# Summing rows, columns and the skip term on TensorE in a state-space output stage

## The chip, the cores and the metric

The kernel runs on one core of a Trainium2 chip. The metric is the device time of the whole program in microseconds. The core has a matrix engine (TensorE, "PE" in the profile, its weight loads "PEld"), VectorE ("DVE"), ScalarE ("ACT"), GpSimd ("POOL") and SyncE ("SP"), which here only issues DMAs. The engines run side by side; each executes its own queue in order, and they wait for each other through semaphores. On-chip tiles lie in SBUF; matmul results lie in PSUM, in banks of 128 partitions by 512 fp32 numbers. All data are fp32.

## The reference, cut to what matters

The input is `x` of 8 images, 96 channels, 128 by 128. Layer 0 normalizes it in groups, runs a convolutional LSTM over its rows and adds the result to `x`. Layer 1 normalizes again, splits each image by a wavelet transform into a low band and three high bands of 64 by 64, sends the low band through a four-direction state-space scan, weighs the high bands by an attention vector, transforms back and adds to its input. The change is in the last lines of the scan (`L` is 4,096, `D_INNER` is 192):

```python
out_y = jnp.moveaxis(ys, 0, -1) + Ds.reshape(K, D_INNER)[None, :, :, None] * xs
inv_y = jnp.flip(out_y[:, 2:4], -1)
wh_y = jnp.swapaxes(out_y[:, 1].reshape(Bn, D_INNER, w, h), 2, 3).reshape(Bn, D_INNER, L)
invwh_y = jnp.swapaxes(inv_y[:, 1].reshape(Bn, D_INNER, w, h), 2, 3).reshape(Bn, D_INNER, L)
y = out_y[:, 0] + inv_y[:, 0] + wh_y + invwh_y
y = jnp.moveaxis(y.reshape(Bn, D_INNER, h, w), 1, -1)
y = _layernorm(y, out_norm_w, out_norm_b)
y = y * jax.nn.silu(z)
return y @ out_proj_w.T
```

Each position of an image therefore gets the sum of the scans along rows (both senses), the scans along columns (both senses), and a skip term: the scan's input times the sum of the four `Ds`. The sum over the 192 inner channels is then layer-normalized, gated by `silu(z)` and projected to 96 channels.

## The kernel before, in words

The program has three stages. First, layer 0 (lines 87 to 224). Second, the scans of all images in turn. Third, a tail, which finishes the last image.

**The scans.** An image has 16 chunks of 512 positions: eight forward (`p` is 0), then the same eight backward. Rows lie in partitions 0 to 63 and columns in 64 to 127 of every scan tile, 64 of the 192 channels at a time (`q` is 0 to 2). A chunk has 24 slots. In a slot two of the 16 states are worked on, 1,024 elements a partition: GpSimd multiplies the input with the B rows (`product`, L1001), ScalarE makes the decays in one of two PSUM buffers (`decay`, L1012), VectorE scans (L1025) and multiplies with the C rows (L1191; every fourth slot GpSimd does it, L1199), and TensorE adds up the states by transposing products against the identity (`add_up`, L1039). SyncE loads B and C rows (`bt`, `ct`, L990) five blocks ahead into rotating tiles. The finished rows and columns go to DRAM as `y_d[b][0]` and `y_d[b][1]`.

**The background.** All other work of neighbouring images is done in the gaps between these instructions: the wavelet analysis and projections of image b+1 (`analysis`, L551), the output stage of image b-1 (`output`, L832) and its inverse transform (`synthesis`, L768). Each of these is a generator (a job) that yields, ahead of every step, its engine, a cost in us, how many rounds it must stay behind the step before (three or more count double), and what it takes or gives of the counted resources: three PSUM banks, twelve `short` tiles of 128 by 512, and some more (`free`, L481). `background` (L1132) is called up to twice a slot, after the scan and before the next one. It gives each engine a budget (TensorE 1.1 us, ScalarE 0.9, VectorE 0.7, GpSimd 1.3, SyncE without limit), and `write` (L488) lets jobs issue steps in order of rank until the budget is gone. Where the scan needs a job's result that has not been issued, `drain` (L538) issues with no limit until it has. All this happens when the program is built; on the chip every engine simply has a fixed order. Synthesis jobs of an image start only when all its output blocks are written out.

**The output stage.** `output` has eight jobs `block(j)` an image, one for each 512 positions, each after the one before. The 192 channels are two parts of 128 and 64 (`parts`). For each part, SyncE loads rows (`y`, L843), columns (`t`, L844), scan input (`u`, L845) and gate (`z`, L846); GpSimd adds columns to rows (L849); VectorE adds the skip term, `u` times the channel's `dsum` (L851). Then, for each part, TensorE multiplies both parts of the sum with `ceny` (identity minus 1/192), which takes the mean off (`pf`, L859); ScalarE squares it (L862) and VectorE multiplies it with the gate (L864). Two more products give the variance (`pv`, L868) and the projection (`po`, L876); ScalarE makes the reciprocal root (L871, L872), VectorE applies it (L879), a last product adds the projected norm bias (`pq`, L883 and L886), and SyncE stores 96 by 512 to `ll_d` (L888).

**Queues.** Loads and stores that SyncE issues stand in one queue; if one has to wait for its buffer, the `bt` and `ct` loads behind it wait too. The weights (`ceny`, `dsum`, `wow`) are made once, at lines 390 to 411. The step vectors' input `dt` of a chunk is loaded by `load_dt` (L926) into one of two buffers and read by three products (L943).

Of the kernel before, what the change touches and what calls it, by code (L numbers as in the profile page):

```python
# [7 lines left out]
F32 = mybir.dt.float32  # L8
# [9 lines left out]
DI = 192  # L18
# [38 lines left out]
def forward_kernel(ctx: ExitStack, tc: tile.TileContext, i, out):  # L57
# [173 lines left out]
    with ExitStack() as s:  # L231
# [163 lines left out]
        for part_i, (d0, m) in enumerate(parts):  # L395
            nc.sync.dma_start(ceny[0:m, part_i, d0:d0 + m], i["ident"][0:m, 0:m])
        nc.vector.tensor_scalar_add(ceny, ceny, -1.0 / DI)
        dsk = wp.tile([128, 2, 4], F32, name="dsk")
        dsum = wp.tile([128, 2], F32, name="dsum")
        onw = wp.tile([128, 2, 2], F32, name="onw")  # L400
# [2 lines left out]
        for part_i, (d0, m) in enumerate(parts):  # L403
            nc.sync.dma_start(dsk[0:m, part_i, :], i["DsT"][d0:d0 + m, :])
            nc.vector.tensor_reduce(dsum[0:m, part_i:part_i + 1], dsk[0:m, part_i, :], AX.X, ALU.add)
            nc.sync.dma_start(onw[0:m, part_i, 0:1], i["out_norm_w"][d0:d0 + m, :])
            nc.sync.dma_start(onw[0:m, part_i, 1:2], i["out_norm_b"][d0:d0 + m, :])
            nc.sync.dma_start(wo[0:m, part_i, :], i["woutT"][d0:d0 + m, :])
            for j in range(2):
                nc.vector.tensor_scalar_mul(wow[0:m, part_i, j, :], wo[0:m, part_i, :],  # L410
                                            onw[0:m, part_i, j:j + 1])

# [63 lines left out]
                    for r in self.give:  # L478
                        free[r] += 1

        free = dict(bank=3, short=NSHORT, raw=2, ph=2, wa=2, yf=2, dl=5)  # L481
        jobs = []
        now, at_slot = [0], [-1]

# [347 lines left out]
        def output(b, begin, end, after):  # L832

            def block(j):
                o = slice(512 * j, 512 * j + 512)
                ys, zs = [], []
                t, u = None, None
                for part_i, (d0, m) in enumerate(parts):
                    yield "SP", 0, (1 if part_i else 0), NONE, NONE
                    if part_i == 0:  # L840
                        t, u = short("t"), short("uo")
                    y, z = short("ysum"), short("zo")
                    nc.sync.dma_start(y[0:m], y_d[b][0, d0:d0 + m, o])  # L843
                    nc.sync.dma_start(t[0:m], y_d[b][1, d0:d0 + m, o])  # L844
                    nc.sync.dma_start(u[0:m], u_d[b][0, d0:d0 + m, o])  # L845
                    nc.sync.dma_start(z[0:m], sz_d[b][d0:d0 + m, o])  # L846
                    ys.append(y), zs.append(z)
                    yield "POOL", 1.3, 3, NONE, NONE
                    nc.gpsimd.tensor_add(y[0:m], y[0:m], t[0:m])  # L849
                    yield "DVE", 1.0, 2, NONE, NONE  # L850
                    nc.vector.scalar_tensor_tensor(y[0:m], u[0:m], dsum[0:m, part_i:part_i + 1], y[0:m],  # L851
                                                   ALU.mult, ALU.add)

                sq, g = (t, ys[1]), (u, ys[0])
                for part_i, (d0, m) in enumerate(parts):
                    yield "PE", 1.72, 1, BANK, NONE
                    pf = ps.tile([m, 512], F32, name="pf", tag="mm")
                    for k_i, (_, k) in enumerate(parts):
                        nc.tensor.matmul(pf, ceny[0:k, k_i, d0:d0 + m], ys[k_i][0:k],  # L859
                                         start=(k_i == 0), stop=(k_i == 1))  # L860
                    yield "ACT", 0.6, 2, NONE, NONE
                    nc.scalar.activation(sq[part_i][0:m], pf, AF.Square)  # L862
                    yield "DVE", 0.68, 2, NONE, BANK
                    nc.vector.tensor_mul(g[part_i][0:m], pf, zs[part_i][0:m])  # L864
                yield "PE", 1.72, 1, BANK, NONE
                pv = ps.tile([C, 512], F32, name="pv", tag="mm")
                for part_i, (d0, m) in enumerate(parts):
                    nc.tensor.matmul(pv, on[0:m, 0:C], sq[part_i][0:m], start=(part_i == 0), stop=(part_i == 1))  # L868
                yield "ACT", 1.3, 2, NONE, BANK
                rs, lo = sq  # L870
                nc.scalar.activation(rs[0:C], pv, AF.Ln, bias=eps[:C])  # L871
                nc.scalar.activation(rs[0:C], rs[0:C], AF.Exp, scale=-0.5)  # L872
                yield "PE", 1.72, 0, BANK, NONE
                po = ps.tile([C, 512], F32, name="po", tag="mm")
                for part_i, (d0, m) in enumerate(parts):
                    nc.tensor.matmul(po, wow[0:m, part_i, 0, :], g[part_i][0:m],  # L876
                                     start=(part_i == 0), stop=(part_i == 1))
                yield "DVE", 0.68, 2, NONE, BANK
                nc.vector.tensor_mul(lo[0:C], po, rs[0:C])  # L879
                yield "PE", 1.72, 1, BANK, NONE  # L880
                pq = ps.tile([C, 512], F32, name="pq", tag="mm")
                for part_i, (d0, m) in enumerate(parts):
                    nc.tensor.matmul(pq, wow[0:m, part_i, 1, :], zs[part_i][0:m],  # L883
                                     start=(part_i == 0), stop=(part_i == 1))
                yield "DVE", 0.68, 2, NONE, BANK
                nc.vector.tensor_add(lo[0:C], pq, lo[0:C])  # L886
                yield "SP", 0, 2, NONE, NONE
                nc.sync.dma_start(ll_d[b][:, o], lo[0:C])  # L888

            done = []  # L890
            for j in range(L // 512):
                done.append(add(begin + (end - begin) * j / (L // 512), block(j), after=[*after, *done[-1:]], urgent=300,
                                take=SHORT * 6, give=SHORT * 6))
            return done
# [31 lines left out]
        def load_dt(ci):  # L926
            b, p, c = chunks[ci]
            yield "SP", 0, 0, NONE, NONE
            dts[ci] = sp.tile([128, CH], F32, name="dt")
            nc.sync.dma_start(dts[ci], dt_d[b][:, c * CH:(c + 1) * CH])  # L930

        def softplus(ci, q):
# [5 lines left out]
            qc = (q + 1) % 3  # L938
            nc.sync.dma_start(du[0:64], u_d[b][0, 64 * q:64 * q + 64, cs])
            nc.sync.dma_start(du[64:128], u_d[b][1, 64 * qc:64 * qc + 64, cs])  # L940
            yield "PE", 0.86, 4, BANK, NONE
            pt = ps.tile([128, CH], F32, name="pt", tag="mm")
            nc.tensor.matmul(pt, dw[:, p, q, :], dts[ci], start=True, stop=True)  # L943
            yield "ACT", 0.62, 2, NONE, NONE
# [169 lines left out]

        now0, dt_job = [0], {}
        ends, att = analysis(0, 0, 0)
        dt_job[0] = add(0, load_dt(0), ends, urgent=1000)
        for q in range(3):
            prepare(0, q, ends)
            hasten(ready[0, q])  # L1120
# [19 lines left out]
        for s in range(total):  # L1140
# [18 lines left out]
            if slot == 0:  # L1159
# [11 lines left out]
                if ci + 1 < len(chunks):  # L1171
                    after = analysed[b + 1][0] if step + 1 == len(order) else []
                    now0[0] = now[0] - halves(s)
                    dt_job[ci + 1] = add(now[0], load_dt(ci + 1), after, urgent=1000)
                    for t in range(3):
                        prepare(ci + 1, t, after)
                if p == 1:
# [99 lines left out]
```

## Time and profile before

| what | value |
|---|---|
| median of three runs | 15,879.47 us (15,873.98 to 15,884.72) |
| the profiled execution's own time | 15,881.9 us |
| its span, first to last instruction | 15,880.1 us |
| mean granted TensorE clock | 0.877 |
| first scan starts, last scan ends | 3,567.9 us, 15,379.0 us |
| TensorE, VectorE, ScalarE, GpSimd busy | 12,017.8, 11,728.4, 8,726.4, 11,270.4 us |
| DMA | 2,239 MB, mean 141 GB/s |

In the rows below, a group is given as line, engine, operation, output and inputs, shapes and count; then its busy time in us, the mean of one instruction in ns, and the idle time of the engine just before, with what ended most of it. A row of a stretch gives start and end, its length, the busy time of PE, PEld, DVE, ACT and POOL with their instruction counts, the granted TensorE clock, the DMA engines' busy share and GB/s. A row of waits gives who waited for whom, total us, how often, and the longest. A timeline row gives start, duration, engine, line, operation and shapes. An fp32 matmul appears as two PE instructions. Shapes such as 64*128 are rows and columns of the weights.

### The profile page before, as it was taken

How to read it: one execution, taken by the hardware profiler on the slowest of the kernel's cores; microseconds unless marked ns; L12 is line 12 of the kernel's file. 1: busy time of each engine (PE TensorE's matmuls, PEld its weight loads, DVE VectorE, ACT ScalarE, POOL GpSimd, SP SyncE). 2: the span in 40 equal slices, each digit the busy share in tenths (PEclk: the TensorE clock that was granted, in tenths of full speed). 3: DMA queues.
4: the chain of work that ended last, by engine and by line, in shares of the span. 5: the costliest groups of instructions: out<-in, count | busy, mean ns of one | idle time of the engine just before them, and what ended most of it. 6: DMA issues, size and time to landing. Idle time of an engine off the chain costs nothing. (4 is left out here: it accounts for less than half of the span.)

```text
span 15880.1 us, 146749 instructions
## 1 busy us (share of the span) xinstructions
PE 12017.8 (76%) x42850; PEld 6570.4 (41%) x42850; DVE 11728.4 (74%) x8612; ACT 8726.4 (55%) x15473; POOL 11270.4 (71%) x9544
## 2 busy tenths in 40 slices
PE   2999999586776777777777777777777777766666
PEld 0444444234444444444444444444444444444432
DVE  4333333209999988998899889888998898899871
ACT  0444444236766665666566656655665566555440
POOL 1333333009899987997798889878987898799760
PEclk9999999788887988888888888888888898877876
DMA  7333333246767777776777777777777777766653
GB/s 166 72 73 72 71 64 66 55 93 167 166 145 164 173 162 157 172 178 153 158 176 170 156 166 174 167 159 164 176 167 156 165 175 164 154 148 145 143 113 78
DMA packets 2458101, 2239.33 MB, mean 141 GB/s; under 512 B 1322929, under 2 KB 1523058, under 8 KB 2457043
## 3 DMA queue, kind: packets, MB, share of 16 engines
q1 hardware_dynamic: 1313491, 2007.56, 54.7%
q10 hardware_dynamic: 1143808, 222.38, 8.5%
q8 instruction: 344, 5.64, 0.2%
q14 instruction: 458, 3.75, 0.1%
HBM read 1862.20 MB, written 367.03 MB: 140 GB/s over the span
## 5 line engine op out<-in xcount | busy, mean ns | idle before, releaser
L1001 POOL TENSOR_TENSOR xb<-du,bt 128x1024 f32<-128x1024 f32 x3072 | 7245.7, 2362 | 330.9 <-DMA bt<-bc_d 169.6
L1025 DVE TENSOR_TENSOR_SCAN da<-da,xb 128x1024 f32<-128x1024 f32 x2304 | 5262.9, 2284 | 377.2 <-ACT da L1012 356.7
L1012 ACT ACTIVATE da<-dl,av 128x512 f32<-128x512 f32 x6144 | 4249.6, 692 | 1044.7 <-DVE hc L1191 494.7
L1039 PE MATMUL py<-ident,hc 128*128 128x128 f32 x18432 | 2882.3, 308 | 2400.6 <-DVE hc L1191 2272.9
L1039 PEld LDWEIGHTS py<-ident,hc 128*128 128x128 f32 x18432 | 2402.5, 159 | 3526.6 <-issue 1478.3
L1191 DVE TENSOR_TENSOR hc<-da,ct 128x1024 f32<-128x1024 f32 x2304 | 2813.2, 1221 | 552.5 <-DMA ct<-bc_d 390.9
L181 PE MATMUL pg<-hx,wq 128*128 128x512 f32 x4608 | 2019.7, 592 | 0.0
L1199 POOL TENSOR_TENSOR xb<-xb,ct 128x1024 f32<-128x1024 f32 x768 | 1809.3, 2356 | 99.3 <-DVE xb L1025 45.6
L1152 ACT COPY carry<-da 128x2 f32<-128x2 f32 x2016 | 319.9, 159 | 2721.8 <-DVE hc L1191 2492.7
L1025 DVE TENSOR_TENSOR_SCAN xb<-da,xb 128x1024 f32<-128x1024 f32 x768 | 1750.1, 2279 | 60.9 <-ACT da L1012 48.3
L584 PE MATMUL pd<-ph,wa 128*128 128x512 f32 x2304 | 1223.2, 663 | 262.7 <-ACT ph L578 142.3
L811 PE MATMUL pd<-ph,wg 128*128 128x504 f32 (+1 forms) x2304 | 1214.1, 659 | 204.5 <-DMA ph<-ll_d 124.4
L181 PEld LDWEIGHTS pg<-hx,wq 128*128 128x128 f32 x4608 | 871.7, 189 | 1106.7 <-issue 1106.3
L198 POOL TENSOR_TENSOR x1b<-xb,hx 96x512 f32<-96x512 f32 x256 | 302.7, 1183 | 1369.7 <-DVE hx L197 1124.4
L186 ACT ACTIVATE gate<-pg,gbias 32x512 f32<-32x512 f32 x768 | 523.3, 681 | 1185.2 <-PE pg L181 1185.2
L644 PE MATMUL pc<-xp,wc 97*128 97x512 f32 x2304 | 1143.6, 627 | 3.4 <-ACT bcs L674 3.4
L1039 PE MATMUL py<-ident,xb 128*128 128x128 f32 x6144 | 1006.5, 318 | 142.4 <-POOL xb L1199 140.5
L1039 PEld LDWEIGHTS py<-ident,xb 128*128 128x128 f32 x6144 | 879.2, 167 | 543.2 <-issue 266.7
L192 DVE TENSOR_TENSOR gate<-gate,gate 96x512 f32<-96x512 f32 x256 | 186.7, 729 | 840.9 <-ACT gate L186 840.9
L584 PEld LDWEIGHTS pd<-ph,wa 128*128 128x128 f32 x2304 | 452.7, 212 | 745.2 <-issue 439.9
L811 PEld LDWEIGHTS pd<-ph,wg 128*128 128x128 f32 x2304 | 461.7, 215 | 677.5 <-issue 580.3
L178 PE MATMUL pg<-x,wq 128*128 128x512 f32 x1536 | 703.4, 594 | 14.7 <-POOL x L168 14.7
(179 smaller groups left out, 12317.9 us busy)
## 6 DMA issues: line engine op xcount, KB each, us to landing
bt<-bc_d SPq DMA_DIRECT2D x2048, 256.0 KB
ct<-bc_d SPq DMA_DIRECT2D x2048, 256.0 KB
raw<-x_d SPq DMA_DIRECT2D x384, 288.0 KB
xb<-in_x SPq DMA_DIRECT2D x64, 1536.0 KB
du<-u_d SPq DMA_DIRECT2D x768, 128.0 KB
wa<-wa_d SPq DMA_DIRECT2D x192, 384.0 KB
xs<-in_x SPq DMA_DIRECT2D x64, 1024.0 KB
x_d<-x1b SPq DMA_DIRECT2D x792, 64.0 KB
```

The lines of the kernel that those rows point to most:

```text
L178: nc.tensor.matmul(pg[m], wq[:, 3, m, :], xk[:, r, bs, 0:W], start=True, stop=False)
L181: nc.tensor.matmul(pg[m], wq[:, tap, m, :], hk[:, r, bs, tap:tap + W], start=False, stop=(tap == 2))
L186: nc.scalar.activation(gg[32 * m:32 * m + 32], pg[m][96:128], AF.Tanh, bias=gbias[96:128, m:m + 1])
L584: nc.tensor.matmul(pd, wa[:, 3 * ty + tx, :], ph[:, ty:ty + 8, tx:tx + W2], start=(ty == tx == 0), stop=(ty == 1 and tx == 2))
L644: nc.tensor.matmul(pc, wc[:, tap, d0:d0 + 128], xp[:, r + ty:r + ty + 8, tx:tx + W2], start=(tap == 0), stop=(tap == 8))
L811: nc.tensor.matmul(pd[:, :, c0:c1], wgs[g][:, 3 * ty + tx, :], ph[:, ty:ty + 8, c0 + tx - 1:c1 + tx - 1], start=(k == 0 and tx == 1), stop ...
L1001: nc.gpsimd.tensor_mul(xb, du.unsqueeze(1).to_broadcast([128, GN, CH]), bcts[k, 0])
L1012: nc.scalar.activation(das[s][:, j], inputs[ci, q][0], AF.Exp, scale=av[:, p, q, n0 + j:n0 + j + 1])
L1025: nc.vector.tensor_tensor_scan(h, da, xb, 0.0, ALU.mult, ALU.add)
L1039: nc.tensor.matmul(pys[key][:, 128 * t:128 * t + 128], hc[:, j, 128 * t:128 * t + 128], ident, is_transpose=True, skip_group_check=True, s ...
L1191: nc.vector.tensor_mul(hc, das[s], bcts[kb, 1])
L1199: nc.gpsimd.tensor_mul(xb, xb, bcts[pk, 1])
```

## The change: what it does

The three sums before the centring product are written into it. The product is linear, so `ceny` times (rows + columns + `dsum` times u) becomes five products that accumulate in one PSUM bank: `ceny` on rows, `ceny` on columns and `cend` on u for the first 128 channels, then one for the last 64 channels' rows and columns stacked in one tile (`yt`), and one for their u. `cend` is `ceny` with its rows scaled by `dsum`. A copy of the last 64 rows of `ceny`, and of `wow`, is put in partitions 64 to 127, where the stacked tiles need them; u and gate of the last 64 channels are stacked too (`uz`). L849 and L851 go. A block now issues its eight loads in one step, makes ten centring matmuls where it made four, and holds two PSUM banks (one for each part) until both parts are squared and gated. To make room for `cend`, the two `dt` buffers become one, with a resource that makes `load_dt` of the next chunk come after the third product of this one.

```diff
         nc.vector.tensor_scalar_add(ceny, ceny, -1.0 / DI)
+        nc.sync.dma_start(ceny[64:128, 1, :], ceny[0:64, 1, :])
+        cend = wp.tile([128, 2, DI], F32, name="cend")
...
             nc.vector.tensor_reduce(dsum[0:m, part_i:part_i + 1], dsk[0:m, part_i, :], AX.X, ALU.add)
+            nc.vector.tensor_scalar_mul(cend[0:m, part_i, :], ceny[0:m, part_i, :], dsum[0:m, part_i:part_i + 1])
...
+        nc.sync.dma_start(wow[64:128, 1, 1, :], wow[0:64, 1, 1, :])
...
-        free = dict(bank=3, short=NSHORT, raw=2, ph=2, wa=2, yf=2, dl=5)
+        free = dict(bank=3, short=NSHORT, raw=2, ph=2, wa=2, yf=2, dl=5, dt=1)
...
-                ys, zs = [], []
-                t, u = None, None
+                yield "SP", 0, 0, NONE, NONE
+                y, t, u, z = (short(n) for n in ("yo", "to", "uo", "zo"))
+                for tile_o, src in ((y, y_d[b][0]), (t, y_d[b][1]), (u, u_d[b][0]), (z, sz_d[b])):
+                    nc.sync.dma_start(tile_o, src[0:128, o])
+
+                yt, uz = short("yt"), short("uz")
+                for tile_o, lower, upper in ((yt, y_d[b][0], y_d[b][1]), (uz, u_d[b][0], sz_d[b])):
+                    nc.sync.dma_start(tile_o[0:64], lower[128:192, o])
+                    nc.sync.dma_start(tile_o[64:128], upper[128:192, o])
+
+                terms = ((0, 128, ceny, y), (0, 128, ceny, t), (0, 128, cend, u), (1, 128, ceny, yt), (1, 64, cend, uz))
+                sq, g, zs = (t, yt), (u, y), (z, uz[64:128])
+                pf = [None, None]
                 for part_i, (d0, m) in enumerate(parts):
-                    yield "SP", 0, (1 if part_i else 0), NONE, NONE
-                    if part_i == 0:
-                        t, u = short("t"), short("uo")
-                    y, z = short("ysum"), short("zo")
-                    nc.sync.dma_start(y[0:m], y_d[b][0, d0:d0 + m, o])
-                    nc.sync.dma_start(t[0:m], y_d[b][1, d0:d0 + m, o])
-                    nc.sync.dma_start(u[0:m], u_d[b][0, d0:d0 + m, o])
-                    nc.sync.dma_start(z[0:m], sz_d[b][d0:d0 + m, o])
-                    ys.append(y), zs.append(z)
-                    yield "POOL", 1.3, 3, NONE, NONE
-                    nc.gpsimd.tensor_add(y[0:m], y[0:m], t[0:m])
-                    yield "DVE", 1.0, 2, NONE, NONE
-                    nc.vector.scalar_tensor_tensor(y[0:m], u[0:m], dsum[0:m, part_i:part_i + 1], y[0:m],
-                                                   ALU.mult, ALU.add)
-
-                sq, g = (t, ys[1]), (u, ys[0])
+                    for n, (k_i, k, weights, rhs) in enumerate(terms):
+                        yield "PE", 0.86, (3 if part_i == n == 0 else 0), (BANK if n == 0 else NONE), NONE
+                        if n == 0:
+                            pf[part_i] = ps.tile([m, 512], F32, name="pf", tag="mm")
+                        nc.tensor.matmul(pf[part_i], weights[0:k, k_i, d0:d0 + m], rhs[0:k],
+                                         start=(n == 0), stop=(n == len(terms) - 1))
                 for part_i, (d0, m) in enumerate(parts):
-                    yield "PE", 1.72, 1, BANK, NONE
-                    pf = ps.tile([m, 512], F32, name="pf", tag="mm")
-                    for k_i, (_, k) in enumerate(parts):
-                        nc.tensor.matmul(pf, ceny[0:k, k_i, d0:d0 + m], ys[k_i][0:k],
-                                         start=(k_i == 0), stop=(k_i == 1))
-                    yield "ACT", 0.6, 2, NONE, NONE
-                    nc.scalar.activation(sq[part_i][0:m], pf, AF.Square)
-                    yield "DVE", 0.68, 2, NONE, BANK
-                    nc.vector.tensor_mul(g[part_i][0:m], pf, zs[part_i][0:m])
+                    yield "ACT", 0.6, (2 if part_i == 0 else 0), NONE, NONE
+                    nc.scalar.activation(sq[part_i][0:m], pf[part_i], AF.Square)
+                for part_i, (d0, m) in enumerate(parts):
+                    yield "DVE", 0.68, (2 if part_i == 0 else 0), NONE, BANK
+                    nc.vector.tensor_mul(g[part_i][0:m], pf[part_i], zs[part_i][0:m])
...
-                    nc.tensor.matmul(pq, wow[0:m, part_i, 1, :], zs[part_i][0:m],
+                    nc.tensor.matmul(pq, wow[128 - m:128, part_i, 1, :], zs[part_i],
...
-            dts[ci] = sp.tile([128, CH], F32, name="dt")
+            dts[ci] = sp.tile([128, CH], F32, name="dt", bufs=1)
...
-            yield "PE", 0.86, 4, BANK, NONE
+            yield "PE", 0.86, 4, BANK, (("dt",) if q == 2 else NONE)
...
-                    dt_job[ci + 1] = add(now[0], load_dt(ci + 1), after, urgent=1000)
+                    dt_job[ci + 1] = add(now[0], load_dt(ci + 1), after, take=("dt",), urgent=1000)
```

More of the change, by code (lines that the diff above doesn't have):

```diff
@@ L1116, in forward_kernel @@
         ends, att = analysis(0, 0, 0)
-        dt_job[0] = add(0, load_dt(0), ends, urgent=1000)
+        dt_job[0] = add(0, load_dt(0), ends, take=("dt",), urgent=1000)
         for q in range(3):
```

## The prediction

> **What bounds the kernel now.** I read the page first, for the busy shares and the costliest groups.
>
> ```profile
> PE 12017.8 (76%) x42850; PEld 6570.4 (41%) x42850; DVE 11728.4 (74%) x8612; ACT 8726.4 (55%) x15473; POOL 11270.4 (71%) x9544
> ...
> L1001 POOL TENSOR_TENSOR xb<-du,bt 128x1024 f32<-128x1024 f32 x3072 | 7245.7, 2362 | 330.9 <-DMA bt<-bc_d 169.6
> L1025 DVE TENSOR_TENSOR_SCAN da<-da,xb 128x1024 f32<-128x1024 f32 x2304 | 5262.9, 2284 | 377.2 <-ACT da L1012 356.7
> ...
> L1191 DVE TENSOR_TENSOR hc<-da,ct 128x1024 f32<-128x1024 f32 x2304 | 2813.2, 1221 | 552.5 <-DMA ct<-bc_d 390.9
> ```
>
> The shares are averages over three stages: the first layer (to about 3,100 us), the scans (3,568 to 15,379 us by the starts of L1025, 3,072 of them, 3.84 us each) and a tail of 501 us after the last scan. The output blocks sit in the last two: 56 of 64 in the scan stage, 8 in the tail. So the next view is one image's scan stage, cut where the output blocks lie (chunks 1 to 5 of image 2) and where the synthesis is bunched (chunks 11 and 12), and what VectorE waited for over that whole image.
>
> ```profile
> 6511.00:6945.60 434.60, 341.96 (x1375) 193.23 (x1376) 417.39 (x273) 298.10 (x559) 413.65 (x361) 0.89 0.73 173
> ...
> 7414.90:7633.70 218.80, 158.28 (x614) 90.11 (x613) 169.02 (x115) 112.98 (x217) 158.01 (x141) 0.86 0.71 148
> ...
> DVE hc L1191 <- DMA ct<-bc_d: 57.3, 17, 12.0
> DVE da L1025 <- ACT da L1012: 53.6, 26, 6.7
> DVE raw L817 <- PE pd L811: 22.7, 15, 4.2
> ```
>
> The columns are PE, PEld, DVE, ACT, POOL busy, clock, DMA share, GB/s. In the output chunks VectorE is busy 417 of 435 us: it sets the pace there, and what leaves its queue shortens them. In chunks 11 and 12 it is busy 169 of 219, and waits for C rows (ct) and for TensorE's synthesis products. GpSimd is nearly as full, but VectorE hardly waits for it.
>
> Third, the groups touched, in the whole execution, then VectorE's in the tail alone (15,385 to 15,630 us).
>
> ```profile
> L859 PE MATMUL pf<-ysum,ceny 128*128 128x512 f32 (+3 forms) x512 | 328.0, 744 | 98.4 <-DVE ysum L851 98.4
> ...
> L851 DVE SCALAR_TENSOR_TENSOR ysum<-uo,dsum,ysum 128x512 f32<-128x512 f32 (+1 forms) x128 | 200.0, 1562 | 105.7 <-POOL ysum L849 105.6
> ...
> L849 POOL TENSOR_TENSOR ysum<-ysum,t 128x512 f32<-128x512 f32 (+1 forms) x128 | 162.1, 1266 | 217.9 <-DMA t<-y_d 214.2 <-PE pf L859 3.1 <-issue 0.2
> ...
> L851 DVE SCALAR_TENSOR_TENSOR ysum<-uo,dsum,ysum 128x512 f32<-128x512 f32 (+1 forms) x16 | 11.9, 747 | 89.7 <-POOL ysum L849 89.7
> ```
>
> L851 takes 0.75 us alone and 1.68 us ((200.0 - 11.9)/112) while GpSimd works. An fp32 matmul is two instructions: x512 is 256 matmuls.
>
> Last, the tail's timeline on TensorE, and its clock.
>
> ```profile
> 15402.56 5.86 PE L859 MATMUL pf<-ysum,ceny 64*128 64x512 f32 x6 [1.97 <-DVE ysum L851]
> 15408.35 2.02 PE L868 MATMUL pv<-t,on 128*96 128x512 f32 x2
> 15410.31 2.02 PE L868 MATMUL pv<-ysum,on 64*96 64x512 f32 x2
> ...
> 15402.60:15420.00 17.40, 17.40 (x18) 3.39 (x18) 2.06 (x3) 2.50 (x4) 0.00 (x0) 0.50 0.00 0
> ```
>
> TensorE works without a break for 17.4 us of each 29.3-us block at half clock, 1.95 us a matmul: in the tail TensorE is the path.
>
> **The change part by part.**
>
> *Sums taken off GpSimd and VectorE, scan stage.* 112 L851 go: 188 us busy; an instruction starts 0.08 us before its predecessor's end (6583.31 + 1.66 against the next start at 6584.90), so 180 us of VectorE's queue. With them goes the wait for L849, 105.6 - 89.7 = 16 us. GpSimd's 112 x 1.27 = 142 us free no path. Sum: -196 us.
>
> *Matmuls added.* Four become ten. From matmul starts in the trace sorted by shape and clock, one instruction takes 0.43 us for 128 rows by 128 columns, 0.53 for 64 by 128, 0.48 for 64 columns; at half clock 0.85, 1.01, 0.91. Old: 3.9 us a block (7.6 at half clock); new: 8 x 0.43 + 0.09 + 2 x 0.53 + 10 x 0.48 = 9.4 us (18.1). At the scan stage's clock of 0.88 (a quarter of the time at half) that is 6.7 us more a block, 375 us in all, beside VectorE's work: chunks 1 to 5 leave TensorE 93 of 435 us idle and get six blocks, 40 us. What may show is the Square (L862): ScalarE would stand there if TensorE is late, with the next decays (L1012) queued behind it and VectorE's scan behind those. Today L862 waits 195.4 us for pf, of which the tail has 164.6 + 25.2: 6 us in the scan stage, so TensorE is on time. Bounds 0 and 56 x 3 = 170; I take +20, near today's row. The first matmul now waits for the loads where GpSimd did; of GpSimd's 217.9 us before L849 the tail has 217.3, so in the scan stage they have always landed: 0.
>
> *Loads.* Eight per block as before, same bytes, but issued in one go (8 x 0.45 = 3.6 us of SyncE against twice 1.8). B and C loads behind them come up to 1.8 us later: 0 to 100 us, +10 taken, since ct waits in these chunks are rare.
>
> *Order.* The planner puts everything else elsewhere. In the order written out for both kernels, image 2's last pf moves from chunk 9 to 6 and the store of its last block from slot 246 to 171; synthesis sums (L817) per chunk from chunk 8 on go from 0, 0, 3, 12, 7, 6, 8, 12 to 4, 4, 6, 6, 8, 4, 11, 5. Slots with 13 or more SyncE issues, where the ct waits of before sit, fall from 61 to 41. A third off 390.9 us of ct waits is 130; slots with 6 or more background matmuls rise from 65 to 90, so I take -100, with ends of +150 (the bunches of ScalarE work, behind 53.6 us of an image's waits, are as many as before and may fall worse) and -280 (half of the ct and pd waits of seven images, 80 us each). Two centring banks are now held together of three; that is in this order, and analysis still ends before the image does (slot 344 against 350).
>
> *One dt buffer, setup.* The order has dt loads at the same slots (22 of the chunk before to 5) and their last reader at 12 to 14 of it: 0; if a load came late the products of the next chunk would wait, a few us per chunk at most. Setup: two copies and two multiplies, 0.6 us an issue on SyncE: +1.
>
> *Tail.* Per block the first matmul starts about 3.8 us after the first load (L849 started 4.4 us after it) instead of 6.6. Then ten pf. [...] By the row all stays at half: 3.8 + 18.1 + 11.3 (pv, po, pq) + 1.6 (last sum, store) = 34.8 us, +44 for 8 blocks. But that run starts with 64-row and 64-column shapes, streaming 1.71 of 1.95 us. Sorted over the trace, 3.4-us steps at half clock with above 80% streaming of full shapes are followed by full clock in over 97 of 100, below 60% in none; full clock is lost only below 50%. The new block opens with four 128x128 matmuls, 6.8 us at half clock without gaps; the same shape in the synthesis got the full clock 3.6 and 4.8 us after a pause. So by the rule: 3.8 + 4.4 at half clock (2.6 matmuls) + 7.2 + 5.9 + 1.6 = 22.9 us, -51. I take the rule's, its shape being the nearest row.
>
> *Sum.* -196 + 20 + 10 - 100 + 1 - 51 = -316 on the span of 15,880: 15,564. The profiled run took 15,881.9 and the median is 15,879.5, so it carries over: **15,560 us**.
>
> **The rivals.**
> 1. *No gain from order, cold tail.* -196 + 44 + 60 (late Squares) = 15,788. For: the planner weighs no waits; against: the ct waits follow SyncE's crowded slots.
> 2. *The even synthesis takes half of those waits.* -280 in place of -100: 15,384. For: chunks 11 and 12 take 108 us each against 85 in chunks 3 to 5; against: 53.6 us of ScalarE waits per image stay.
> 3. *TensorE late, slower.* At L862 ScalarE stands until the tenth matmul, the decays behind it. It decides from 316/56 = 5.6 us a block on; at 8 us the time is 15,564 + 448 = 16,012. For: at half clock a block wants 18 us plus 0.21 x 8 per transposed slot, and the planner counts 8.6; against: such a backlog fills TensorE above 80% and so brings the full clock.
> 4. *It does nothing:* VectorE's freed time turns into waits for ct or decays; 15,870. Against: chunks 1 to 5, 96% busy.
>
> **How the numbers follow.** Sum as worked out 0.47 (15,470 to 15,650), rival 1 0.22, rival 2 0.15, rival 3 0.13, rival 4 0.03. A measurement tells 0.2% (32 us) from nothing. Faster 0.84, same 0.03, slower 0.13. Range: from rival 2 to a little above rival 1, 15,380 to 15,840; outside are rival 3, rival 4 and a little below.
>
> **What would show it.** L849 and L851 gone and 1,280 pf instructions; VectorE busy about 200 us less; chunks 1 to 5 still over 95% busy and some 14 us shorter; ct waits near 260 us; L862's waits in the scan stage under 40 us; tail blocks near 23 us with a clock that reaches 1.0 in each. Wrong if the waits for decays (L1012) grow by more than 200 us, or if the tail stays at 0.50.

## The result and the profile after

The changed kernel takes 15,697.77 us (median; 15,690.29 to 15,712.49), the kernel before 15,882.09 us beside it: a ratio of 0.9888, 95% interval 0.9875 to 0.9900. It is 1.1% faster, by 184 us where 320 were forecast. The profiled execution has a span of 15,702.6 us against 15,880.1, so 177.5 us are there to be found.

The page of the changed kernel, busy shares and the same three groups:

```profile
PE 12169.3 (77%) x43618; PEld 6616.4 (42%) x43618; DVE 11561.5 (74%) x8486; ACT 8727.7 (56%) x15473; POOL 11082.0 (71%) x9416
...
L1002 POOL TENSOR_TENSOR xb<-du,bt 128x1024 f32<-128x1024 f32 x3072 | 7238.8, 2360 | 332.2 <-DVE da L1026 167.1
L1026 DVE TENSOR_TENSOR_SCAN da<-da,xb 128x1024 f32<-128x1024 f32 x2304 | 5265.7, 2285 | 384.0 <-ACT da L1013 355.8
...
L1192 DVE TENSOR_TENSOR hc<-da,ct 128x1024 f32<-128x1024 f32 x2304 | 2816.4, 1222 | 535.4 <-DMA ct<-bc_d 365.6
```

VectorE's busy time fell by 167 us. The wait for C rows (`ct`), which the forecast put near 260 us, is 366: it hardly moved from 391.

The same stretches of image 2 as before, chunks 1 to 5 and then 11 and 12 (start and end, length, busy PE, PEld, DVE, ACT, POOL, clock, DMA share, GB/s):

```profile
6490.10:6923.90 433.80, 358.89 (x1445) 192.68 (x1444) 405.35 (x266) 295.51 (x557) 396.96 (x349) 0.93 0.75 181
7391.80:7603.00 211.20, 155.98 (x606) 92.03 (x605) 167.37 (x114) 118.66 (x226) 160.28 (x142) 0.85 0.71 148
```

In chunks 1 to 5 VectorE has 405 us of work where it had 417, yet the stretch is 0.8 us shorter, not 14: the share of busy time fell from 96% to 93%. Chunks 11 and 12 are 7.6 us shorter. The means over images 1 to 6 are steadier: chunks 1 to 5 take 433.2 us (437.3 before), chunks 11 and 12 together 213.1 (216.0), of which chunk 12 alone grew, from 107.5 to 115.4.

The whole tail before and after, in the same columns:

```profile
15379.00:15880.00 501.00, 313.91 (x462) 97.90 (x460) 68.06 (x97) 28.80 (x47) 20.12 (x16) 0.63 0.31 74
15253.40:15702.60 449.20, 303.59 (x560) 110.07 (x558) 56.17 (x82) 28.90 (x47) 0.00 (x0) 0.80 0.35 83
```

The second and the start of the third block of the new tail on TensorE (the first column is the start, the second the duration):

```profile
15293.65 2.05 PE L858 MATMUL pf<-yo,ceny 128*128 128x512 f32 x2 [4.87 <-DMA yo<-y_d]
15295.49 1.63 PE L858 MATMUL pf<-to,ceny 128*128 128x512 f32 x2
15296.96 1.02 PE L858 MATMUL pf<-uo,cend 128*128 128x512 f32 x2
...
15299.82 1.07 PE L858 MATMUL pf<-yo,ceny 128*64 128x512 f32 x2
...
15315.92 2.05 PE L858 MATMUL pf<-yo,ceny 128*128 128x512 f32 x2 [5.29 <-DMA yo<-y_d]
15317.76 1.91 PE L858 MATMUL pf<-to,ceny 128*128 128x512 f32 x2
15319.47 1.59 PE L858 MATMUL pf<-uo,cend 128*128 128x512 f32 x2
15320.89 1.02 PE L858 MATMUL pf<-yt,ceny 128*128 128x512 f32 x2
```

A pair of matmul instructions begins at 2.05 us, half clock, and is at 1.02 us, full clock, from the third pair on in the second block and from the fourth in the third. In blocks 2 to 8 the full clock comes 3.0 to 6.1 us after the block's first matmul, 4.8 us on average. The blocks' stores come 22.9 us apart on average, where they came 29.7 us apart.

The span of every kernel is cut in the next table at the first scan's start and the last scan's end. "Idle" are VectorE's gaps of over 150 ns in the scan stage, by what ended them.

| kernel | span | scan stage | tail | VectorE busy in scan stage | idle: `ct` | idle: ScalarE | idle: TensorE | idle: GpSimd |
|---|---|---|---|---|---|---|---|---|
| before | 15,880.1 | 11,811.1 | 501.1 | 10,509.9 | 398.8 | 481.2 | 210.7 | 37.5 |
| changed | 15,702.6 | 11,688.1 | 449.2 | 10,354.1 | 367.6 | 544.7 | 228.8 | 13.0 |
| x1, sums left out of the old kernel | 15,708.2 | 11,669.7 | 467.9 | 10,335.8 | 429.1 | 489.6 | 216.6 | 21.8 |
| x2, four of the ten products | 15,662.6 | 11,668.2 | 428.0 | 10,352.6 | 381.1 | 490.9 | 234.2 | 33.9 |
| x3, new block in the tail only | 15,815.3 | 11,799.5 | 444.9 | 10,509.1 | 374.4 | 466.5 | 230.5 | 47.7 |

So 123 us come from the scan stage and 52 from the tail; 2.5 stand in what comes before the first scan. The prediction had 266 for the scan stage's steps and 51 for the tail.

### The profile page after: what moved, and what is told of

It reads as the page before. It is cut to its first block, busy times and chain, and to the rows that moved or that the text cites. A ratio compares the mean times of both kernels' runs of the same rounds, so it can differ in the third digit from the quotient of the medians.

```text
span 15702.6 us, 147935 instructions
## 1 busy us (share of the span) xinstructions
PE 12169.3 (77%) x43618; PEld 6616.4 (42%) x43618; DVE 11561.5 (74%) x8486; ACT 8727.7 (56%) x15473; POOL 11082.0 (71%) x9416
## 5 line engine op out<-in xcount | busy, mean ns | idle before, releaser
L1040 PE MATMUL py<-ident,hc 128*128 128x128 f32 x18432 | 2831.3, 304 | 2205.3 <-DVE hc L1192 2113.2
L1040 PEld LDWEIGHTS py<-ident,hc 128*128 128x128 f32 x18432 | 2365.9, 157 | 3304.4 <-issue 1631.2
```

Source lines behind the costliest of these rows:

```text
L1040: nc.tensor.matmul(pys[key][:, 128 * t:128 * t + 128], hc[:, j, 128 * t:128 * t + 128], ident, is_transpose=True, skip_group_check=True, s ...
```

## The experiments

Three further groups of runs follow the first four, each with its own runs of the kernel before (15,905, 15,872 and 15,864 us, against 15,873 for the first): ratios compare across groups, and so do differences within one. Each profile is of one execution, and executions of one scan stage differ: x4 below, whose scan stage is the changed kernel's, had 11,667.8 us against 11,688.1; in the second group the same scan stage had 11,712.6 (y1) and 11,730.7 (x5). Its `ct` waits were 360 us in x4, 368 in the changed kernel, 387 in y1 and 412 in x5. A difference of 20 us within a group, or of 40 between groups, says nothing by itself.

### What the two removed sums were worth, in the old order

```diff
-                    nc.gpsimd.tensor_add(y[0:m], y[0:m], t[0:m])
...
-                    nc.vector.scalar_tensor_tensor(y[0:m], u[0:m], dsum[0:m, part_i:part_i + 1], y[0:m],
-                                                   ALU.mult, ALU.add)
```

> The kernel before with GpSimd's and VectorE's two sums (L849, L851) left out and every planner step kept, so that the order of all else is that of before; rows alone are normalized (columns and skip term are missing from the result). My theory, that VectorE sets the pace and the sums cost what they occupy: scan stage 11,811 to about 11,650 us, tail 501 to about 465, total about 15,685. Rival, that VectorE's freed time turns into other waits at once: scan stage above 11,750, total above 15,780.

Measured: 15,709.22 us, ratio 0.9900 [0.9885, 0.9915]; the scan stage is 141 us shorter, not 196. Waits of VectorE over the scan stage in this kernel (total us, times, longest):

```profile
DVE hc L1188 <- DMA ct<-bc_d: 425.3, 114, 12.6
DVE da L1022 <- ACT da L1009: 362.0, 179, 7.1
DVE raw L817 <- PE pd L811: 176.7, 106, 7.2
```

VectorE has 174 us less to do and waits 28 us more (1,139.8 to 1,167.5 us in all): for `ct` 30, for ScalarE 8 and for TensorE 6 more, for GpSimd 16 less. The C rows come when they come; a VectorE that arrives earlier waits longer. Even in chunks 1 to 5, where nine L851 an image are gone (VectorE's busy time 402 us where it had 417, means of images 1 to 6), the stretch is only 8.4 us shorter, and `ct` waits there went from 6 to 12 us. Some 5 us more of the stage are gaps under 150 ns. They fit a latency that an L851 between a scan and its product hid: the product starts 2.38 us after its scan's start, an L851 did so after 2.20.

### Ten products against four, in the new order

```diff
+                        if n in (0, 3):
-                        nc.tensor.matmul(pf[part_i], weights[0:k, k_i, d0:d0 + m], rhs[0:k],
-                                         start=(n == 0), stop=(n == len(terms) - 1))
+                            nc.tensor.matmul(pf[part_i], weights[0:k, k_i, d0:d0 + m], rhs[0:k],
+                                             start=(n == 0), stop=(n == 3))
```

> The changed kernel with four of its ten centring matmuls a block issued, all planner steps and loads kept, so the order is the changed kernel's (columns of the first part and skip terms are missing from the result). Theory A, that the added matmuls hide beside VectorE and the new order is what took time back: scan stage 11,688 to 11,670 to 11,690. Theory B, that the added TensorE work makes ScalarE's decays late: scan stage below 11,640. Tail: 449 to about 405 where any gapless shape brings the clock, still about 450 where only full shapes do.

Measured: 15,663.29 us, ratio 0.9868 [0.9853, 0.9883]. This kernel and x1 do the same amount of work on every engine in nearly all their instructions; they differ in the order. Their scan stages differ by 1.5 us. The new order does lower the `ct` waits (429 to 381), but VectorE has 17 us more of busy time and 18 us more of waits for TensorE. The order, from which the prediction took 100 us, gave nothing that can be told from the 20 us between two executions.

The changed kernel stands 34 us behind this one, 21 of them in the tail: the six further products of a block cost some 13 us in the scan stage by the times, 20 by these two profiles, and nothing by x4's, whose scan stage of 11,667.8 us has them too. They do not show at the Square (L862), whose waits there are 0.5 us. They show in the waits for ScalarE, which are 545 us with them (535 in x4) and 491 without. VectorE's waits for the decays, without them and with them:

```profile
DVE da L1027 <- ACT da L1014: 319.1, 172, 7.7
DVE da L1026 <- ACT da L1013: 355.8, 188, 7.9
```

What delays the decays was not taken apart.

### The new block in the tail alone

The first seven images get the old block, the last one the new; `dt` has one buffer.

> Images 0 to 6 with the old output block, the last image's eight blocks with the new one; one dt buffer as in the changed kernel. My theory: scan stage 11,811 as before within 15 us (the single dt buffer is free), tail 449 as in the changed kernel, total 15,828. Rival, that the single dt buffer costs: scan stage above 11,830.

Measured: 15,814.38 us, ratio 0.9962 [0.9948, 0.9976]; a tail of 444.9 us and a scan stage of 11,799.5. The tail's gain is the block's own and owes nothing to the scan stage, and the single `dt` buffer costs nothing.

### What warms TensorE: the width of the product

```diff
-                for part_i, (d0, m) in enumerate(parts):
+                for step, part_i in enumerate((1, 0) if b == B - 1 else (0, 1)):
```

In the tail the five 64-column products come first.

> The changed kernel, in the tail's eight blocks the five 64-column matmuls first and the five 128-column ones after them; scans untouched. If only full shapes bring TensorE to the full clock: the first 9 us of each block stay at half clock, a block takes some 5 us longer, tail 449 to about 490. If any gapless run of matmuls does (streaming above 80% of a 3.4-us step): tail within 12 us of 449.

Measured: 15,710.11 us, ratio 0.9896 [0.9881, 0.9910], and a tail of 456.1 us:

```profile
15236.40:15692.00 455.60, 304.67 (x560) 106.86 (x558) 56.11 (x81) 27.87 (x47) 0.00 (x0) 0.80 0.34 82
```

The clock is 0.80, as in the changed kernel's tail, and in blocks 2 to 8 it is full 5.2 to 5.8 us after the block's first product, while the 64-column products still run. Products of 64 columns bring the full clock as well as those of 128: the prediction's "full shapes" was too narrow.

### What warms TensorE: the rows of the product

```diff
+                if b == B - 1:
+                    terms = ((0, 128, ceny, y), (1, 64, ceny, yt), (0, 128, ceny, t),
+                             (1, 64, ceny, yt), (0, 128, cend, u), (1, 64, cend, uz))
```

In the tail, products over 128 and over 64 rows come by turns; the last 64 channels' rows are counted twice and their columns are left out in the last image.

> The changed kernel, whose last image's blocks make twelve centring products with 128 and 64 rows by turns (the last 64 channels' rows are counted twice there in place of their columns). Over the traces so far, a matmul with 64 weight rows seems to count about half toward the full clock, and one with 64 columns in full. If so the alternation, like the old tail's, never gets the full clock: 3.8 + 22.9 + 11.3 + 1.6 = 39.6 us a block, tail near 575 us, clock 0.50 there. If rows don't matter: about 25.5 us a block, tail near 462.

Measured: 15,884.52 us, ratio 0.9986 [0.9977, 0.9995]; a tail of 595.5 us. Its first 348 us and the whole:

```profile
15301.50:15650.00 348.50, 282.99 (x302) 57.66 (x300) 23.21 (x33) 22.67 (x36) 0.00 (x0) 0.51 0.18 45
15301.50:15897.00 595.50, 438.69 (x590) 123.20 (x588) 56.13 (x81) 28.79 (x47) 0.00 (x0) 0.61 0.26 62
```

TensorE is 81% busy for 348 us and stays at 0.51. Gapless products over 128 rows brought the full clock within 6.1 us in the changed kernel's tail; alternating with 64 rows did not bring it in 348 us. Products over 64 rows alone were not tried. The old tail, at half clock for 256 us, has the same alternation in its centring products, in `pv`, `po` and `pq`. Nearly all of those 256 us, in the kernel before:

```profile
15385.40:15637.00 251.60, 156.90 (x160) 31.41 (x160) 33.92 (x48) 22.14 (x36) 20.12 (x16) 0.50 0.25 63
```

With the full clock the tail of this run would have taken 462 us by the expectation's estimate; by that the slow clock cost 134.

### GpSimd's sum alone

```diff
-                    nc.gpsimd.tensor_add(y[0:m], y[0:m], t[0:m])
```

> The kernel before without GpSimd's sum (L849) alone, planner steps kept (columns are missing from the result). If VectorE is what sets the pace: scan stage 10 to 40 us shorter than 11,811 (the wait for L849, and a quicker L851 where GpSimd no longer works on the same tiles), so most of the 141 us of leaving out both belongs to L851. If GpSimd sets it: over 100 us shorter. Tail about 20 us shorter.

Measured: 15,886.64 us, ratio 0.9985 [0.9977, 0.9992], with a tail of 494.1 us. About 18 us are gained by the times, 7 of them in the tail. The expected 10 to 40 us of the scan stage can't be read from the profile: it has 11,834.3 us, and no kernel before was profiled in this group. By the times nearly all of x1's gain is VectorE's instruction. GpSimd's freed 142 us gave next to nothing, as the prediction had it; the VectorE sum became slightly faster, 1.50 us a piece against 1.56.

### A later analysis: does `ct` follow the crowded slots?

```diff
-                        analysed[b + 1] = analysis(b + 1, now[0] + 4, now[0] + 0.71 * IMAGE)
+                        analysed[b + 1] = analysis(b + 1, now[0] + 4, now[0] + 0.8 * IMAGE)
```

> The changed kernel with the analysis of the next image spread over 0.80 of an image instead of 0.71; nothing else. Slots with 13 or more SyncE issues fall from 41 to 23. If waits for C rows follow such slots, as my prediction had it: those waits fall from 368 to below 280 us and the scan stage from about 11,680 to about 11,590. If the order only moves waits from one releaser to another: scan stage within 30 us of 11,680.

Measured: 15,930.3 us, ratio 1.0015 [1.0008, 1.0022], slower than the kernel before. VectorE's waits:

```profile
DVE hc L1192 <- DMA ct<-bc_d: 473.7, 150, 11.3
DVE da L1026 <- ACT da L1013: 354.1, 169, 8.6
```

Slots with 13 or more SyncE issues fell from 41 to 23, and the `ct` waits rose to 474 us (387 and 412 in y1 and x5, the same group with the changed order); the scan stage is 11,930.4 us, some 200 longer than theirs. The measure on which the order term rested does not predict them.

### What delays the C rows: one DMA more in SyncE's queue

VectorE waits for a `ct` load at 114 of its products in the changed kernel. There the load was issued 5.3 us (median) before the product wanted it, and a `ct` load takes 7.1 us to land (median): SyncE was late with it. SyncE's and ScalarE's DMAs take turns on eight completion semaphores (1,368 or 1,369 DMAs on each in the changed kernel, where 9,319 of SyncE's 9,729 wait for their own semaphore, themselves or in an instruction just ahead), and SyncE often stands, with all loads behind it, until the DMA before on the same semaphore has landed (786 times in the changed kernel's scan stage, 1,536 us). Three kernels add DMAs without adding any bytes or moving any other instruction. First, one of the synthesis block's two `raw` loads in two halves; then both; then, in place of these, the last of its four output stores in two halves.

```diff
                 for k in range(2):
-                    nc.sync.dma_start(xr[32 * k:32 * k + 32], x1_d[b, g, 2 - 2 * k:4 - 2 * k, :, 8 * j + k:8 * j + k + 8, :]
+                    for q0, nq in (((0, 1), (1, 1)) if k in (0,) else ((0, 2),)):
+                        nc.sync.dma_start(xr[32 * k + 16 * q0:32 * k + 16 * (q0 + nq)], ...
```

> The changed kernel, with one of the two raw loads of every synthesis block issued as two DMAs of half the size: one more SyncE DMA per block (384 in all), same bytes, every engine's order of instructions unchanged otherwise. Theory P (a SyncE DMA stands until an unrelated DMA that shares its completion semaphore has landed, and which ones meet is set by how many DMAs lie between them): the waits for ct, 368 us in the changed kernel, move by more than 60 us in one direction or the other, the stores that SyncE stood at (y_d<-y at L824, 118 us) are replaced by others, and the time moves with them, by 30 to 200 us. Theory C (SyncE is crowded, each issue costs about 0.45 us): 384 x 0.45 = 173 us of SyncE, of which a part shows: ct waits 370 to 420 us, the time 0 to 50 us longer. Theory N (neither matters): within 20 us of the changed kernel in the waits and within 30 in the time.

> The same with both raw loads split: two more DMAs per synthesis block (768). Theory P: ct waits again more than 60 us from 368, with no relation to those of the kernel with one more, on either side. Theory C: twice the effect of one more load: ct waits 370 to 470 us, the time 0 to 100 us longer. Theory N: as the changed kernel.

> The changed kernel with the last of the four out stores of every synthesis block issued as two: as many SyncE DMAs as in the kernel with one more load, but the added one stands at the other end of the block. Theory C: the same as with one more load, within 20 us in ct waits. Theory P: different from it by more than 40 us in ct waits, since the pairs inside the block differ. Theory N: as the changed kernel.

The expectations count 384 blocks; there are 192, of which 168 lie in the scan stage. Measured:

| kernel | DMAs added in the scan stage | time, ratio | scan stage | `ct` waits | SyncE stands for a landing |
|---|---|---|---|---|---|
| changed | 0 | 15,697.77, 0.9888 | 11,688.1 | 367.6 | 1,536 |
| one more store | 168 | 15,748.33, 0.9924 [0.9908, 0.9941] | 11,722.4 | 404.8 | 1,664 |
| one more load | 168 | 15,793.85, 0.9953 [0.9938, 0.9968] | 11,779.9 | 453.4 | 1,582 |
| two more loads | 336 | 15,893.51, 1.0013 [1.0006, 1.0020] | 11,871.1 | 549.4 | 1,577 |

The last column is worked out from the trace: SyncE idle for over 0.3 us directly before a DMA's issue, until at most 0.3 us after the last landing mark of the DMA before on the same semaphore. Where an instruction that only waits stands before the issue, its idle time is not counted; with it the changed kernel has some 2,500 us. The two-load kernel's row of waits:

```profile
DVE hc L1194 <- DMA ct<-bc_d: 545.7, 124, 14.4
DVE da L1028 <- ACT da L1015: 364.7, 188, 8.0
```

Theory C's numbers are too small. Its shape is there: twice the DMAs cost twice the time, 92 and 183 us, nearly all of it in the `ct` waits. The price is 0.55 us for each added load (92/168), more than its whole issue (0.42 us for a `raw` load of this block), where the expectation let only a part show. An added store costs 0.20 us by the profiles (34 us in all, within what two groups differ by) and 0.30 by the ratios, whose intervals do not meet; its two halves take 0.32 us each to issue where the whole took 0.43, and each half leaves nine landing marks where the whole left 16. So whether its place, its kind or its shorter issue makes it cheaper is open.

Theory P's bounds hold, but they were wide: both loads moved the `ct` waits by over 60 us, and the store lies 49 us from one load. The stores that it named stayed (77 us of stands for `y_d` in the changed kernel's list of waits, not 118; 123 and 115 with more loads), and the sum of the stands hardly moved with more loads (1,536, 1,582, 1,577). One row speaks for it, though: SyncE's stands at the synthesis block's `raw` loads for the landing of a `y_d` store, in the changed kernel, with one more load and with two:

```profile
SPq L804 <- DMA y_d<-y: 9.3, 5, 2.4
SPq L805 <- DMA y_d<-y: 95.6, 19, 8.8
SPq L805 <- DMA y_d<-y: 174.0, 31, 9.2
```

They grow by 86 and 165 us, about as much as the time. So an added load costs about 0.55 us here, but these runs do not tell whether it costs that by its issue or by the landing it has to stand for.

### The opposite: fewer loads

```diff
-            nc.sync.dma_start(du[0:64], u_d[b][0, 64 * q:64 * q + 64, cs])
-            nc.sync.dma_start(du[64:128], u_d[b][1, 64 * qc:64 * qc + 64, cs])
+            blocks = u_d[b].rearrange("k (n d) l -> (k n) d l", d=64)
+            nc.sync.dma_start(du, blocks[q:4 + qc:3 + qc - q, :, cs])
...
+                nc.sync.dma_start(yt, y_d[b][:, 128:192, o])
```

This kernel also has the overlapped tail that follows below.

> The kernel with the overlapped tail, with 448 fewer DMAs in SyncE's queue and the same bytes: the two halves of each du (384 pairs) and of each yt (64 pairs) come in one DMA each. If every SyncE DMA in the scan stage has a price of 0.09 us (measured for one more store) to 0.24 us (for one more load), all of it in waits for ct: ct waits fall from the changed kernel's 368 us by 40 to 108, the scan stage from 11,688 us to 11,580 to 11,650, and the time lies 40 to 108 us below the overlapped tail's 0.9849 of before (0.978 to 0.982). If the price depends on where the DMA stands and du's stand where no ct load is near: ct waits 350 to 390 us, ratio 0.983 to 0.987. If which DMAs meet on a completion semaphore matters more than their number: ct waits off by more than 60 us to either side, the time with them.

Measured: 16,174.56 us, ratio 1.0198 [1.0181, 1.0215]: by the ratios some 550 us above the kernel with the overlapped tail alone. `ct` waits are 630 us and waits for ScalarE 739. The row of SyncE's waits that grew (over the scan stage, here to 15,500 us), in the changed kernel and here, and the load in the list of DMAs:

```profile
SPq L991 <- DMA du<-u_d: 14.1, 10, 5.0
SPq L993 <- DMA du<-u_d: 336.0, 77, 8.7
```

```profile
du<-u_d SPq DMA_DIRECT2D x384, 256.0 KB
```

The expectation's prices of 0.09 and 0.24 us rest on the 384 blocks, too. In the trace nearly every DMA leaves 16 landing marks on its semaphore (in the changed kernel's, 174,682 marks for 10,945 DMAs). Two of three merged `du` (`q` of 0 and 1) leave three and land after 12.1 us (median), where each half took 5.7; the merged `yt` leaves three too and lands after 12.7 instead of 5.7. The third merged `du` (`q` of 2), whose two blocks lie side by side and so form one of 128 rows, leaves 16 and lands after 6.8. What comes next on the same semaphores stands for the slow ones: SyncE's stands for its own DMAs went from 523 us in the changed kernel to 1,104. The third `du`, one DMA of the same bytes, is the control: 6.8 us with 16 marks from blocks side by side, against 12.1 us with three from separate ones. What in a separate source makes a DMA slow was not shown. So this run did not test the price of a DMA; it made the DMA slow. What it shows is that slow landings raise the `ct` waits too, from 387 us in the kernel with the overlapped tail to 630.

### A version that beats both: overlap the tail's blocks

```diff
-                done.append(add(begin + (end - begin) * j / (L // 512), block(j), after=[*after, *done[-1:]], urgent=300,
+                done.append(add(begin + (end - begin) * j / (L // 512), block(j),
+                                after=[*after, *(done[-2:-1] if b == B - 1 else done[-1:])], urgent=300,
...
-                    done.append(add(at(j), block(g, j), after=[*after, wt[g]], take=("raw", "ph"), give=("raw",)))
+                    done.append(add(at(j), block(g, j), after=[*after, wt[g], *outs[max(2 * j - 1, 0):2 * j + 3]],
+                                    take=("raw", "ph"), give=("raw",)))
...
-        drain(synthesis(B - 1, now[0], now[0], [*outs, analysed[B - 1][1]]))
+        drain(synthesis(B - 1, now[0], now[0], [analysed[B - 1][1]], outs))
```

For the last image an output block may start beside the one before it, and a synthesis block waits only for the output blocks that it reads.

> The changed kernel, in the tail alone two output blocks under way at a time, and each synthesis block waiting only for the output blocks whose rows it reads. Scans as in the changed kernel. If the tail is bound by TensorE once it is filled (about 122 + 124 us at full clock): tail near 340, total near 15,590. If by loads and the two ph and raw buffers: tail above 400, total above 15,645.

Measured: 15,667.32 us, ratio 0.9849 [0.9834, 0.9864], against 0.9888 for the changed kernel. The tail is 378 us:

```profile
15281.50:15452.00 170.50, 143.90 (x305) 43.83 (x304) 25.42 (x38) 23.00 (x37) 0.00 (x0) 0.96 0.44 104
15452.00:15659.00 207.00, 133.69 (x256) 54.42 (x254) 30.42 (x45) 5.79 (x10) 0.00 (x0) 0.80 0.39 90
```

While output blocks overlap, TensorE is 84% busy at a clock of 0.96. The synthesis behind them leaves it idle for 73 of 207 us, in waits for loads, and the clock falls to 0.80. The tail of 378 us lies between the two expectations.

## Why the prediction was right, and where it was not

The sign, the range and the tail hold. The size does not: 316 us were summed, the profile shows 177.5. The measured 15,698 us lies outside the 15,470 to 15,650 given to the sum as worked out; it is in the range because the range reaches past rival 1.

| step | forecast | shown | by |
|---|---|---|---|
| L851 and the wait for L849 leave VectorE | -196 | -141 | x1 against before, scan stage |
| order, and loads in one go | -100 + 10 | -1.5 | x2 against x1, scan stage |
| six more products a block | +20 | +20 (some 13 by the times, 0 by x4's profile) | changed against x2 |
| setup | +1 | -2.5, no more than one kernel's spread | changed against before |
| tail | -51 | -52 | changed against before, and x3 |

**The step that failed is "Order".** It took a third off the `ct` waits because slots with 13 or more SyncE issues fell from 61 to 41. Image 2's synthesis did become more even, but the waits did not follow: y2 emptied those slots further and waited longer. A `ct` load is late by what stands ahead of it in SyncE's queue at that moment: further DMAs (0.20 to 0.55 us of time for each, w1 to w3), and SyncE's stands for landings (m1). Where no DMA is added or merged, stands and waits go together loosely: 1,490 us and 381 in x2, 1,536 and 368 in the changed kernel, 1,609 and 399 before, 1,721 and 429 in x1, 1,859 and 474 in y2, but also 1,526 and 360 in x4, 1,576 and 374 in x3, 1,558 and 387 in y1, 1,581 and 412 in x5, 1,581 and 437 in x6. That is an association, and apart from y2 much of it is within the spread of one scan stage; no run changed the stands alone, so how much of the waits they cause stays open. So does the question which property of the order could have been counted in their place.

**The removal was sized by VectorE's queue alone.** The queue's part nearly held: 174 us of busy time, 16 us of waits for GpSimd. The prediction's own row of waits already showed that in this kernel VectorE also waits for `ct`, decays and synthesis products; x1 gives 44 us back to these three. This is rival 4's mechanism at a quarter of its size. The mistake was to take chunks 1 to 5, 96% busy, as a sign that freed time meets no other limit. It met one there too: with 15 us of work gone, they became 8.4 us shorter in x1, in the old order.

**The products cost what was said, at another place.** The Square never waited, as forecast; rival 3 did not come. The `pf` products take 313 us more in the scan stage (265 to 577; 375 were forecast), TensorE as a whole is busy 164 us more at a clock of 0.87, and waits for ScalarE grew. That the price came out at +20 is partly luck: two executions differ by as much.

**The tail came out within 1 us, for a reason that was half right.** The forecast said that a block which opens with full shapes gets the full clock, after 4.4 us. No run shows the 4.4 us, which were an estimate; in blocks 2 to 8 of the new tail the full clock came after 3.0 to 6.1 us, 4.8 on average. x4 shows that 64 columns do as well as 128 (5.2 to 5.8 us), x5 that 64 rows by turns with 128 do not (0.51 for 348 us). Work without a break was not enough by itself: in the old tail 17.4 us of it stayed at 0.50. Had I gone by the old tail's row alone, the forecast of the tail would have been 96 us too long (44 and 52).

**Rivals.** Rival 1 has half of it right: there was no gain from order; its cold tail did not come. Its 15,788 is 90 us above the result, the forecast 138 below: the rival was nearer. Rival 2 is out. Of the things that were to show it, L849 and L851 are gone, five groups of 256 `pf` instructions stand in their place, L862 waits 0.5 us in the scan stage, and all waits for ScalarE grew by 63 us, those for decays by less than the 200 that would have spoken against the forecast; the `ct` waits and the chunks missed.

## What to carry to other kernels

When the bounding engine also waits, take an instruction off its queue and count what it waits for next: here about a quarter of the freed time (44 of 190 us) came back as waits. Do not put a number on a new order from a count of crowded slots unless two orders have been seen to obey that count; zero, with a range, would have been the better term. Where one queue issues both the loads on the path and everything else, DMAs added to it had a price (0.20 to 0.55 us each), and merging two of them lost where the merged one landed later (after 12.1 us in place of 5.7).

## What the runs showed of the hardware

- Gapless products over 128 rows, of 128 columns, got the full clock after 3.0 to 6.1 us (changed kernel's tail), and blocks that begin with 64 columns after 5.2 to 5.8 (x4); a TensorE 81% busy with 128 and 64 rows by turns stayed at 0.51 for 348 us (x5). In the traces of the kernel before and of the changed one, 528 and 471 stretches of half clock last whole multiples of 3.41 us; only the last of each, which reaches past the program's end, does not. An estimate from a fit over such steps of six of these traces (6,365 steps at half clock, 97% of them sorted rightly): a 64-row product counts as about half of a 128-row one, and the clock rises after a step of which products, so weighted, fill 0.76 or more.
- In the changed kernel's trace the 10,945 DMAs of SyncE and ScalarE are spread over eight completion semaphores, 1,368 or 1,369 on each. In the scan stage SyncE stood, directly before an issue, until the landing of the DMA before on the same semaphore: 252 times for ScalarE's DMAs (1,013 us) and 534 times for its own (523 us).
- A 256-KB load from two separate blocks of 64 rows in one DMA took 12.1 us to land and left three landing marks; from two blocks side by side it took 6.8 us and left 16 (m1). A half of such a load, as a DMA of its own, took 5.7 us (changed kernel).
